# Layer 0 of a two-layer network on Trainium2: all columns of the transform matrices in x's first two steps

## The chip, the cores and the metric

The kernel runs on one core of a Trainium2 chip. The metric is the device time of one execution in microseconds (us), the median of a few runs. A profile of one further execution gives the start and end of every instruction on the engines: TensorE (PE matmuls, PEld weight loads), VectorE (DVE), ScalarE (ACT), GpSimd (POOL) and SyncE (SP, which issues most transfers), and the clock that was granted to TensorE.

## The reference

The input x is 4 batches of 32 images (times) of 128 x 128, in float32. Layer 0 is a convolution in Fourier space with an attention over the 32 times of a batch, two more spectral layers and several normalizations; layer 1 is an attention over 1024 tokens of 128 channels and a mixture of experts. Only the start of layer 0 bears on this case: x is normalized by groups of channels (`_gn`) and by image (`_inorm`), and the low modes of its two-dimensional Fourier transform are taken:

```
xn = _inorm(xa, norm1_w, norm1_b)
X = jnp.fft.rfft2(x, norm='forward')
Xk = jnp.concatenate([X[:, :, :mh, :mw], X[:, :, -mh:, :mw]], axis=2)
Yk = jnp.einsum('bixy,ioxy->boxy', Xk, w)
...
scores = jnp.einsum('bntk,bnsk->bnts', qf, kf) / (np.float32(np.sqrt(Hs * Ws)) * temperature)
p_attn = jax.nn.softmax(scores, axis=-1)
```

The keys, queries and values of the attention are spectral convolutions of the same image, so that their scores can be formed from the modes of x.

## The kernel before

**Transforms as matmuls.** A transform of an image is two matmuls with constant matrices. In the first step (`half_rows`, L285) the image is the stationary operand, 128 x 128, and the moving operand is `rows`, a matrix of 128 columns: 64 cosines and 64 sines of the frequencies 0 to 31 and -32 to -1. As the input is real, frequencies 0 to 32 are enough, and the step takes the first 33 columns of each half, 66 in all (L293). Four images go into one PSUM tile `pz`; ScalarE copies 32 columns of each half to `z` (L297) and the 33rd to `z32` (L298), and after two such tiles adds a constant to one column (L589). In the second step (`columns_of`, L495) two images' parts of `z` are the stationary operand, 128 x 128, and the moving operand is `colg`, cosines and sines of 33 frequencies along the other axis, times the group scale: 101 columns, of which the step takes the first 68 (L502). Four such matmuls fill the PSUM tile `it`, which ScalarE copies to `fold` (L507). `edge_row` (L562) takes other columns of `colg` for `z32`. All operands are float32.

**The stages of `spectra_of_images` (L481).** The 32 images of a batch are four groups of eight. For each group come two `pz` tiles, their copies, and then the second step of the group before. After the second step of two groups `unfold` (L509) makes the modes of 16 images: matmuls `em` (L521) and `std` (L532, L535), from which VectorE writes `xe`, `xm` (L537), two rows of biases (L544, L545) and `xx` (L548). `image_weights` (L465) makes the scale of each image: the sum `my` on TensorE, then a root (the helper `inv_std`, ScalarE at L248 and L251, VectorE at L247 and L252 to L255). After it comes `attention_weights` (L645): ScalarE copies `xe` to PSUM as `xp` (L655), VectorE and GpSimd form products `pa` and `pb` (L685, L687), and TensorE sums them (`so` L669, `sp` L700).

**What stands beside it.** For batch 0 these stages run alone at the start of the kernel, behind the loads of x and the group sums (`rows8`, L398; `bg`, L380), with the preparation of weights on VectorE: `value_weights` (L605 to L619) and the weights of keys and queries, `w_re` and `w_im` (L819 to L834). ScalarE also makes a selection matrix, `picked` (L628). For batches 1 to 3 they run at the end of the batch before, behind the second mode multiplication of its spectral layers (`spectra`, L1084: first step `pz` L305, second step `px` L1106, the multiplication on VectorE at L1117 and L1120 and its sum on GpSimd at L1123; ScalarE negates a part of it at L1068). Between them stand the coefficients of that batch's last normalization (`coefficients`, L1257): energies on VectorE (L1074, L1082), two sums `ms` on TensorE (L380), and two roots, r1 and rm, on ScalarE and VectorE, with short VectorE operations from L1266 to L1284.

**Order.** Layer 1 has a schedule written by hand (L1842). Layer 0 hasn't: a scheduler gives the instructions of each engine their order from its own estimates of their times, from the order of the program, and from the dependences that `behind` adds by hand. An engine then takes its instructions in that order. `pz` and the sums `my` share two PSUM buffers (tag "a"), `it` and others two (tag "b"), `em` and `std` two of double size (tag "wide").

Of the kernel before, what the change touches and what calls it, by code (L numbers as in the profile page):

```python
# [7 lines left out]
F32 = mybir.dt.float32  # L8
# [5 lines left out]
P = 128  # L14
B, T, H, C = 4, 32, 128, 128
NH = 32
KX, KY = 64, 33
KA = 17
KP = 9
GI = 8  # L20
# [76 lines left out]
NX = 2 + 3 * KY  # L97
# [33 lines left out]
def layer0(  # L131
    tc, x, kq_modes, kq_mirror, v_modes, v_mirror, pcw, mcols, mrows, heads, heads_by_row, heads_row, small_row, by_p, inv_cols, dram, x1, first
):
    nc = tc.nc
# [7 lines left out]
    const, ps, images, values, modes = (p.__enter__() for p in pools + right)  # L142

    def behind(later, earlier):

        tc.add_manual_dep(
            later.ins,
            earlier.ins.name,
            mybir.DependencyInfo(mybir.DependencyClass.NoSync, mybir.DependencyReason.DATA),
            reason="order",  # L150
        )
# [25 lines left out]
    def columns(n):  # L177
        at[0] += n
        return cst[:, at[0] - n : at[0]]

    rows = columns(128)
# [103 lines left out]
    def half_rows(images, z, last):  # L285

        for k in range(0, GI, 4):
            pz = ps.tile([P, 4, 2, KY], F32, name="pz", tag="a")
            for j in range(4):
                mm = nc.tensor.matmul(  # L290
                    pz[:, j],
                    images[k + j],
                    rows.rearrange("p (r x) -> p r x", r=2)[:, :, :KY],  # L293
                    start=True,
                    stop=True,
                )
            nc.scalar.copy(z[:, k : k + 4], pz[:, :, :, :32])  # L297
            nc.scalar.copy(last[:, :, k : k + 4], pz[:, :, :, 32].rearrange("p t r -> p r t"))  # L298
        return mm
# [181 lines left out]
    def spectra_of_images(b, xt, normed, then=None):  # L481


        _, colg, shift, sv, _ = normed
        n = 1 + KY
# [5 lines left out]
        half = T // 2  # L491
        pairs = half // 2
        folded = {}

        def columns_of(g, z):  # L495

            if g % half == 0:
                folded[g // half] = grp.tile([P, pairs, 2 * n], F32, name="fold", tag="fold")
            it = ps.tile([P, GI // 2, 2 * n], F32, name="it", tag="b")
            for j in range(GI // 2):  # L500
                mm = nc.tensor.matmul(
                    it[:, j], z[:, 2 * j : 2 * j + 2].rearrange("p t r x -> p (t r x)"), colg[:, : 2 * n], start=True, stop=True  # L502
                )
                if g == GI and then is not None:
                    behind(mm, summing["ms"])
            k = g % half // 2
            nc.scalar.copy(folded[g // half][:, k : k + GI // 2], it)  # L507

        def unfold(a):  # L509

# [71 lines left out]
        for g in GROUPS:  # L582
            z = grp.tile([P, GI, 2, 32], F32, name="z", tag="z")
            made = half_rows([xt[:, g + t] for t in range(GI)], z, z32[:, :, g : g + GI])
            if g == 0:
                ysc, scaled = image_weights(sv, made)
            if g == GI and then is not None:
                then(made)
            nc.scalar.activation(z[:, :, 0, 0], z[:, :, 0, 0], AF.Identity, bias=shift)  # L589
            if waiting:  # L590
                columns_of(*waiting.pop())
            if g == 3 * GI:
                unfold(0)
            waiting.append((g, z))
        columns_of(*waiting.pop())
        edges = edge_row()
        unfold(1)
# [228 lines left out]
    for dst, a, c, op in (  # L826
# [3 lines left out]
        t = prep.tile(shape, F32, name="wt", tag="wt")  # L830
# [64 lines left out]
    for b in range(B):  # L895
# [49 lines left out]
        for x0 in range(0, KX, NK):  # L945
# [3 lines left out]
            for i in range(4):  # L949
# [16 lines left out]
                for k in range(2):  # L966
# [11 lines left out]
                    for j in range(4):  # L978
# [4 lines left out]
                            start=i == 0 and k == 0,  # L983
                            stop=i == 3 and k == 1,
# [20 lines left out]
        for y0 in range(0, KY, 8):  # L1005
            n = min(8, KY - y0)
            py = ps.tile([P, 8, 2, T], F32, name="py", tag="b")
            for k in range(n):
                for part in range(2):
# [4 lines left out]
                        start=True,  # L1014
                        stop=True,
# [209 lines left out]
        for g in range(1, 4):  # L1225
            gelu(1, g)
            h, k = divmod(4 * g - 4, GI)
# [781 lines left out]
```

## Time and profile before

| | us |
|---|---|
| runs (3) | 2968.66, 2972.97, 2974.31; median 2972.97 |
| the profiled execution's own time | 2970.21 |
| its span, first to last instruction | 2968.5 |
| layer 0, to the first work of layer 1 on its path | about 850 |
| mean granted clock of TensorE | 0.979 |

The page shows TensorE busy for 2754.0 us (93% of the span), ScalarE for 2323.7, VectorE for 2187.5 and GpSimd for 2028.2. Most of it is layer 1, which starts near 830 us and which the change does not touch. So the busy shares of the whole say little here; what counts is which engine each stage of layer 0 waits for. In the list of groups each line has source line, engine, operation, output and inputs with their shapes, the count, busy time and mean of one in ns, and then the idle time ahead of them with what ended it. A float32 matmul stands there as two records. The chain of waits gives start, length and name of each piece of the path that ended last.

### The profile page before, as it was taken

The page shows a single profiled execution, that of the slowest core. Times are in us where ns is not written, and L with a number is a line of the kernel's source. Part 1 is how long each engine was busy: PE and PEld are TensorE (multiplying, and loading weights), DVE is VectorE, ACT ScalarE, POOL GpSimd, SP SyncE. Part 2 cuts the span into 40 slices and gives each one's busy share as a digit, 9 for nine tenths or more (in the row PEclk, how much of TensorE's full clock was granted, in tenths as well). Part 3 has the DMA queues.
Part 4 walks back from the last instruction along what each step waited for, and adds up shares of the span by engine and source line. Part 5 has one row for each costly group of instructions (what it writes and reads, how often), then busy time and mean ns, then how long its engine had stood idle before and what let it go on. Part 6 is the DMA issues. An engine that isn't in the chain of part 4 may idle for free.

```text
span 2968.5 us, 52711 instructions
## 1 busy us (share of the span) xinstructions
PE 2754.0 (93%) x19506; PEld 1364.1 (46%) x19506; DVE 2187.5 (74%) x4934; ACT 2323.7 (78%) x3235; POOL 2028.2 (68%) x1801
## 2 busy tenths in 40 slices
PE   8888988988878999999899999989999999999997
PEld 5465564664644443344444343444444343444443
DVE  4876787778866677775678688667778766878877
ACT  3554555456359999899899999989999998999991
POOL 1703605417208987878987878898787889798773
PEclk8998999999989999999999999999999999999998
DMA  3403304205021101002010100111010020000000
GB/s 93 126 1 70 117 1 106 81 9 152 14 61 33 33 1 40 8 16 57 1 26 15 26 15 8 42 25 31 15 26 15 10 56 15 26 13 21 15 15 14
DMA packets 151154, 107.72 MB, mean 36 GB/s; under 512 B 36303, under 2 KB 140018, under 8 KB 150898
## 3 DMA queue, kind: packets, MB, share of 16 engines
q1 hardware_dynamic: 147633, 102.26, 13.3%
q8 instruction: 154, 2.52, 0.4%
q10 hardware_dynamic: 3264, 2.10, 0.3%
q14 instruction: 103, 0.84, 0.1%
HBM read 63.86 MB, written 19.50 MB: 28 GB/s over the span
## 4 chain that ended last, share of the span: by engine, by line
PE 60%; POOL 12%; ACT 11%; DVE 10%; issue 6%; DMA 0%; POOLq 0%; DVEq 0%; ACTq 0%
PE d L1799 20%; PE po L1818 11%; PE px L1705 6%; ACT r L1849 5%; PE n L1799 4%; POOL e L1858 3%; PE po L909 3%; POOL e L1857 3%; POOL u L972 2%; ACT e L1865 2%; DVE r L1854 2%; POOL kx L1464 2%; PE pz L305 2%; DVE xc L1709 1%; PE px L1106 1%
## 5 line engine op out<-in xcount | busy, mean ns | idle before, releaser
L1854 DVE TENSOR_TENSOR r<-n,r 128x1024 f32<-128x1024 f32 (+1 forms) x1056 | 961.5, 952 | 478.6 <-PE n L1799 391.1
L1857 POOL TENSOR_TENSOR e<-r 128x512 f32<-128x512 f32 x528 | 674.0, 1277 | 270.2 <-DVE r L1854 269.6
L1849 ACT ACTIVATE r<-d 128x1024 f32<-128x1024 f32 (+1 forms) x1056 | 793.4, 803 | 64.7 <-PE n L1799 56.8
L1861 ACT ACTIVATE r<-r 128x1536 f32<-128x1536 f32 x528 | 783.6, 1484 | 16.7
L1858 POOL TENSOR_TENSOR e<-e,r 128x512 f32<-128x512 f32 x528 | 671.6, 1272 | 41.4
L1799 PE MATMUL d<-qe,ke 32*128 32x512 f32 (+3 forms) x2304 | 606.4, 602 | 39.4 <-ACT r L1849 35.0
L1818 PE MATMUL po<-e,kx 128*128 128x512 f32 (+3 forms) x1152 | 594.8, 605 | 17.4 <-POOL e L1870 17.4
L1799 PE MATMUL n<-qe,ke 32*128 32x512 f32 (+3 forms) x2304 | 606.3, 602 | 0.0
L1799 PE MATMUL n<-qf,kf 32*128 32x512 f32 (+3 forms) x2304 | 553.1, 555 | 0.0
L1799 PE MATMUL d<-qf,kf 32*128 32x512 f32 (+3 forms) x2304 | 551.8, 555 | 0.0
L1709 DVE SCALAR_TENSOR_TENSOR xc<-px,wgt,xc 128x128 f32<-128x128 f32 x1024 | 358.0, 350 | 42.1 <-PE px L1705 10.6
L1865 ACT ACTIVATE e<-e 128x512 f32<-128x512 f32 x528 | 325.8, 617 | 66.6 <-POOL e L1858 65.7
L1818 PEld LDWEIGHTS po<-e,kx 128*128 128x128 f32 x1152 | 175.8, 188 | 395.2 <-issue 309.7
L1799 PEld LDWEIGHTS d<-qe,ke 32*128 32x128 f32 x2304 | 176.6, 183 | 358.8 <-ACT r L1849 339.1
L1799 PEld LDWEIGHTS d<-qf,kf 32*128 32x128 f32 x2304 | 220.5, 186 | 175.7 <-issue 163.4
L1705 PE MATMUL px<-we,x2t 128*128 128x512 f32 x512 | 265.7, 605 | 6.7 <-DVE xc L1709 5.5
L972 POOL TENSOR_TENSOR u<-xb,gb 128x858 f32<-128x858 f32 (+1 forms) x112 | 219.7, 1994 | 56.9 <-PE po L909 53.3
L1799 PEld LDWEIGHTS n<-qf,kf 32*128 32x128 f32 x2304 | 228.3, 185 | 19.5 <-issue 11.7
L1123 POOL TENSOR_TENSOR spec<-part,part 128x512 f32<-128x512 f32 x16 | 25.3, 1578 | 304.0 <-DVE part L1120 110.8
L976 DVE TENSOR_TENSOR u<-xw,gb 128x858 f32<-128x858 f32 (+1 forms) x208 | 214.8, 1101 | 5.1 <-PE po L909 2.9
L1799 PEld LDWEIGHTS n<-qe,ke 32*128 32x128 f32 x2304 | 177.6, 183 | 9.4 <-DVE r L1854 0.9
L909 PE MATMUL po<-u,pr 128*32 128x429 f32 (+1 forms) x1280 | 150.4, 525 | 27.3 <-POOL u L972 17.7
(421 smaller groups left out, 3398.5 us busy)
## 6 DMA issues: line engine op xcount, KB each, us to landing
xb<-xd SPq DMA_DIRECT2D x128, 214.5 KB
xc<-x SPq DMA_DIRECT2D x29, 512.0 KB
x<-x SPq DMA_DIRECT2D x16, 512.0 KB
qf<-qe SPq DMA_DIRECT2D x64, 128.0 KB
out<-xc SPq DMA_DIRECT2D x15, 512.0 KB
x<-in_x SPq DMA_DIRECT2D x14, 512.0 KB
xb<-xd SPq DMA_DIRECT2D x32, 198.0 KB
kf<-ke SPq DMA_DIRECT2D x32, 128.0 KB
```

The source lines that it names most:

```text
L909: mm = nc.tensor.matmul(*args, **kw)
L972: weighed = nc.gpsimd.tensor_tensor(u, xb, gk, ALU.mult)
L1705: nc.tensor.matmul(px, x2t[:, k * P : (k + 1) * P], we[:, e0 : e0 + 4], start=True, stop=True)
L1709: nc.vector.scalar_tensor_tensor(xc[:, k], px[:, e], wgt[:, k, e0 + e : e0 + e + 1], xc[:, k], ALU.mult, ALU.add)
L1799: nc.tensor.matmul(o, k, q, start=turn == 0 or g > 0, stop=turn == 1 or g > 0)
L1818: nc.tensor.matmul(sums[c, h][:, q0 : q0 + c1 - c0], kx[:, jb], e[:, c0:c1], start=jb == 0, stop=is_last and q0 > 2 * P, skip_group_check= ...
L1849: nc.scalar.activation(r[:, g], d, AF.Ln, scale=1.0 / DSCALE)
L1854: nc.vector.tensor_tensor(r[:, g], part, r[:, g], ALU.mult)
L1857: nc.gpsimd.tensor_tensor(e, r[:, 1], r[:, 2], ALU.add)
L1858: nc.gpsimd.tensor_tensor(e, e, r[:, 0], ALU.add)
L1861: nc.scalar.activation(r, r, AF.Exp, scale=-1.0)
L1865: nc.scalar.activation(e, e, AF.Exp)
```

## The change

The first step takes all 128 columns of `rows`, and the second all 101 columns of `colg`. The tiles `pz` and `it` grow to hold them. The copies take the same elements as before: from `pz` the columns 0 to 31 and 32 of each half, from `it` the first 68 of 101 columns.

```diff
     def half_rows(images, z, last):
 
         for k in range(0, GI, 4):
-            pz = ps.tile([P, 4, 2, KY], F32, name="pz", tag="a")
+            pz = ps.tile([P, 4, 2, KX], F32, name="pz", tag="a")
             for j in range(4):
                 mm = nc.tensor.matmul(
                     pz[:, j],
                     images[k + j],
-                    rows.rearrange("p (r x) -> p r x", r=2)[:, :, :KY],
+                    rows.rearrange("p (r x) -> p r x", r=2),
                     start=True,
                     stop=True,
                 )
...
-            it = ps.tile([P, GI // 2, 2 * n], F32, name="it", tag="b")
+            it = ps.tile([P, GI // 2, NX], F32, name="it", tag="b")
             for j in range(GI // 2):
                 mm = nc.tensor.matmul(
-                    it[:, j], z[:, 2 * j : 2 * j + 2].rearrange("p t r x -> p (t r x)"), colg[:, : 2 * n], start=True, stop=True
+                    it[:, j], z[:, 2 * j : 2 * j + 2].rearrange("p t r x -> p (t r x)"), colg, start=True, stop=True
                 )
...
-            nc.scalar.copy(folded[g // half][:, k : k + GI // 2], it)
+            nc.scalar.copy(folded[g // half][:, k : k + GI // 2], it[:, :, : 2 * n])
```

As the scheduler's estimates depend on sizes, the order of instructions changes too, on TensorE, VectorE and ScalarE, in the stages named above and nowhere else; GpSimd's and SyncE's stay. In batch 0 VectorE's work for `w_re` and `w_im` (L820 to L834) comes ahead of the first `xe` (L537) instead of between its rows, and ScalarE's root of the image scale ahead of the second copy of group 1. In batches 1 to 3 ScalarE's part stands so (batch 2, from the two programs' lists; g0 to g3 are the groups of images, a and b their two tiles):

```
before: copies g0a g0b | copy g1a | fold g0 | negation L1068 | copy g1b | copy g2a | root n1 | copy g2b | root r1 | fold g1 | copies g3a g3b | fold g2 | xe L547 | root rm | fold g3
after:  copies g0a g0b | negation L1068 | copy g1a | fold g0 | root n1 | copy g1b | copy g2a | root r1 | copy g2b | fold g1 | copy g3a | root rm | copy g3b | fold g2 | xe L547 | fold g3
```

On TensorE the two sums `ms` stand after the first tile of group 2 instead of inside the last tile of group 3, and on VectorE most of the coefficients ahead of the first `xe` of the batch instead of between its rows.

## The prediction

> **What bounds the kernel now.** I read the page first, then the list of groups with shapes kept apart, then the chain of waits over layer 0 (the first 860 us of 2968.5), and last the busy time of each engine in stretches of 3.41 us, because the granted clock of TensorE moves in that step.
>
> The changed instructions are small. In the group list they stand beside a neighbour of the same weights with 128 columns:
>
> ```profile
> L305 PE MATMUL pz<-cst,q 128*128 128x128 f32 x256 | 36.5, 285 | 1.4 <-ACT z L225 1.4
> L290 PE MATMUL pz<-cst,x 128*128 128x66 f32 x256 | 39.1, 312 | 2.1 <-ACT z L298 2.0
> L290 PEld LDWEIGHTS pz<-cst,x 128*128 128x128 f32 x256 | 36.8, 227 | 4.4 <-ACT z L298 3.0 <-issue 1.4
> L501 PE MATMUL it<-colg,z 128*128 128x68 f32 x128 | 19.6, 306 | 0.0
> ```
>
> 128 images give 256 records at L290 and 64 pairs give 128 at L501: each f32 matmul is two passes. 66 columns cost no less than 128 (312 against 285 ns of one). The chain of waits says where they are on the path; nearly all of it is in batch 0:
>
> ```profile
> 22.45 3.43 PE pz L290 x16
> 26.40 1.97 PE pz L290 x8
> 28.37 1.71 PE it L501 x8
> 30.08 5.12 PE pz L290 x24
> 35.20 1.71 PE it L501 x8
> 36.91 3.41 PE pz L290 x16
> 40.32 1.71 PE it L501 x8
> 42.03 1.17 PE em L521 x32
> ```
>
> 24 passes in 5.12 us are 213 ns each; in batch 3 the weight loads of 32 passes start at 647.84 and the next matmul's at 651.41, 112 ns each. The factor is the clock. Columns of the next view: length of the stretch, then busy us and instructions of PE, PEld, DVE, ACT, POOL, then PEclk.
>
> ```profile
> 21.66:25.07 3.41, 3.28 (x16) 3.31 (x16) 2.20 (x13) 0.44 (x2) 0.00 (x0) 0.50 0.00 0
> 25.07:28.48 3.41, 3.30 (x16) 3.11 (x15) 2.15 (x11) 0.79 (x4) 0.00 (x0) 0.50 0.00 0
> 38.72:42.14 3.42, 3.42 (x21) 3.29 (x23) 0.00 (x0) 1.16 (x6) 0.00 (x0) 0.50 0.00 0
> 42.14:45.55 3.41, 3.41 (x42) 2.36 (x40) 2.24 (x9) 2.54 (x4) 0.00 (x0) 0.50 0.00 0
> 45.55:48.96 3.41, 3.15 (x52) 2.67 (x53) 2.74 (x12) 0.59 (x2) 0.00 (x0) 1.00 0.39 60
> 632.64:636.06 3.42, 3.41 (x16) 3.41 (x17) 2.10 (x10) 0.00 (x0) 0.00 (x0) 0.50 0.01 2
> 636.06:639.47 3.41, 3.41 (x39) 2.48 (x39) 2.88 (x6) 0.66 (x2) 0.00 (x0) 1.00 0.02 5
> ```
>
> From 21.66 to 45.55 us, seven stretches, TensorE runs at half clock although it is busy throughout. In batch 3 one such stretch is enough. The two are alike but for one thing: 21.66:25.07 holds 2 passes of bg (L380) and 14 of L290 with 66 columns; 632.64:636.06 holds 2 passes of bg and 14 of L305 with 128 columns. After the second the clock is full; after the first it stays at half.
>
> [...] half-clock stretches are 1, 2, 3, 4 or 7 times 3.41 us. [...] The trace has 112 ns a pass at full clock, 213 at half: [...]
>
> **The change, part by part.**
>
> Matmul time: 128 matmuls at L290 and 64 at L501, each two passes. New pass 112 ns at full clock and 213 at half, as L305 has with 128 columns; 101 lies between. Cost 0. [...]
>
> Copies at L297, L298, L507: same elements, other strides in PSUM (33 to 64, 68 to 101). L297, which already reads with strides, takes 375 ns for 256 elements a partition, L507, contiguous today, 390 for 272. I take 0; at 30 ns for each of 80 copies it would be 2.4 us, mostly beside TensorE. [...]
>
> The clock in batch 0, the main term. With 128 columns 21.66:25.07 becomes the twin of 632.64:636.06: [...] So the clock is full from 25.07. Until then 13.2 of L290's 64 passes are done. Before em (L521) follow 50.8 of L290, 24 of L501 and 2 of my: 76.8 x 0.112 = 8.6 us, plus 0.5 us where group 1 waits for the copies of group 0 (0.45 in batch 1). em starts at 34.2, not 41.96. Behind it I laid the new order end to end with the old durations. VectorE's order in the changed program has the w_re/w_im work (L820 to L834, about 3.5 us), which today stands between the xe rows, ahead of xe: its earlier work ends near 32.0 (today's 3.5 us from 32.73, brought forward because ACT's new order does n_r behind the first copy of group 1), so xe follows at 35.5, today 43.26. ACT copies picked (L628, 2.13 us) from 34.8 to 36.9, then xe's tail, then the last fold by 37.6; em of the second half ends near 38.6, xe at 38.7, xm and the bias rows to 39.3, xp on ACT to 39.9, the first pa (L685) at 39.95. Today it starts at 49.71: 9.8 us gained, and the chain from there to 82 us is TensorE back to back, so it moves along. No transfer holds it: DMA is at 0.00 to 0.02 from 21.66 to 45.55.
> Another execution has another phase. The rise falls between 24.8 and 28.2; at 28.5 I get 8.4, at 31.9, [...] 6.7. I take 9.0.
>
> The order of batches 1 to 3, which the instruction lists of both programs show to move; POOL and SP keep theirs. On ACT the negation L1068, which waits for POOL's spec (L1123), now stands ahead of group 1's first copy instead of behind a later one; on TensorE the two sums ms stand after 9 to 12 fewer matmuls; on VectorE nearly all of the coefficients (L1266 to L1281) come ahead of the first xe. The first costs: POOL ends at 238.08, 443.54, 646.63, the copy could start at 238.37, 442.91, 645.56, so with 0.6 us of L1068 TensorE stalls about 0.4, 1.0 and 1.5 us. Against it, today's own stall before group 2 (0.67 us in batches 2 and 3) goes, and the sums come 1 to 2 us earlier, with them the root r and rm, on whose ACT round trip VectorE waits 1.1 + 0.6 us in batch 2. Laid end to end, the last xe comes at 251.6, 456.3, 659.6 for 251.26, 456.96, 659.61, and the bias rows after it are no longer mixed with cq: pa moves by -0.1, -0.8, -0.2. I take -1.1, between -3 and +4 (stalls kept, gains lost).
>
> Sum: 2970.2 (the profiled execution's own time; span 2968.5) - 9.0 - 1.1 = 2960.1. The median of the runs, 2972.97, is 2.8 above that execution; with it 2963.
>
> **Rivals.** What this measurement can tell from no change is 0.2%, 5.9 us.
> (A) The clock rises one or two windows into batch 0: 2963. For: the twin windows. [...]
> (B) [...] the clock stays at half: only the order is left, 2972. [...] Against: L305 alone raised it in batch 3.
> (C) Slower: ACT's negation. If the stall ahead of group 1's copy (0.4 to 1.5 us) isn't absorbed by the earlier sums, and the roots r and rm, now ahead of the last copies of groups 2 and 3, hold TensorE too, each of three batches loses 2 to 3 us; with a clock as in B that is 2980. It decides from 2.0 us a batch. For: these waits are new. Against: the sums are the later end in batches 2 and 3 today.
> (D) The clock rises, but VectorE, with 3.5 us of w_re ahead of xe, or ACT's picked is slower than laid out, and half of the gain is lost: 2968.
>
> **How the numbers follow.** A 0.70, B 0.15, C 0.09, D 0.06. Predicted 2963. The range takes A with its phases (gain 12 [...] to 6.7), D and the nearer half of B: 2956 to 2972. Faster by over 0.2% is A: 0.70; within: B and D, 0.21; slower: C, 0.09.
>
> **What would show it.** PEclk 1.00 in most of 26 to 42 us; L290 passes of 112 ns from group 1 on; the first pa in batch 0 near 40 us; L290 and L501 with the old mean at equal clock. Wrong if the clock stays at 0.50 to 40 us, if a pass takes more than 112 ns at full clock, or if the first pa of batches 1 to 3 comes over 1.5 us later within its batch.

## The result, and the profile after

The changed kernel takes 2957.74 us (median of 6 runs, 2956.24 to 2960.34); the kernel before took 2973.64 us beside it (2968.66 to 2978.81). The ratio is 0.995, with a 95% interval of 0.9937 to 0.9963: 11 to 19 us faster. The two profiled executions, 2957.97 and 2970.21 us, are 12.2 us apart.

The chain of waits of the changed kernel in batch 0 follows (start us, us, what; "..." marks pieces left out). From the first L290, at 21.75 us, to em it needs 12.7 us; the kernel before needed 19.7.

```profile
21.96 3.53 PE pz L290 x16
...
25.52 0.37 ACT z L297
...
26.01 1.34 PE pz L290 x8
...
29.11 1.81 PE pz L290 x16
30.92 0.87 PE it L501 x8
31.80 1.81 PE pz L290 x16
33.60 0.87 PE it L501 x8
34.48 0.75 PE em L521 x29
```

16 passes of L290 take 1.81 us here and took 3.41; em starts at 34.4 us and started at 41.96. The next view is the busy time by stretches of 3.41 us, called windows from here on. Its columns are those of the prediction: length, then busy us and instructions of PE, PEld, DVE, ACT and POOL, then PEclk.

```profile
19.59:23.00 3.41, 1.70 (x8) 1.73 (x9) 2.41 (x16) 0.27 (x2) 0.00 (x0) 0.50 0.00 0
23.00:26.42 3.42, 3.21 (x16) 3.02 (x16) 1.64 (x10) 1.16 (x5) 0.00 (x0) 0.50 0.00 0
26.42:29.83 3.41, 3.41 (x32) 3.41 (x32) 3.33 (x17) 1.83 (x8) 0.00 (x0) 1.00 0.02 5
29.83:33.24 3.41, 3.41 (x33) 3.41 (x33) 3.41 (x17) 1.99 (x8) 0.00 (x0) 1.00 0.01 2
```

After the first window that is filled with 128-column passes, 23.00 to 26.42 us, the clock is full, and a window holds 32 passes instead of 16. Before, seven windows in a row stayed at half clock, TensorE busy for 3.28 to 3.42 us of each. The groups of the changed instructions:

```profile
L290 PE MATMUL pz<-cst,x 128*128 128x128 f32 x256 | 36.4, 292 | 2.5 <-ACT z L298 2.4
...
L501 PE MATMUL it<-colg,z 128*128 128x101 f32 x128 | 17.2, 275 | 0.0
```

One of them is not dearer with more columns, but cheaper: 292 ns for 312 at L290 and 275 for 306 at L501. More of them run at full clock.

The two profiled executions can be divided at the first L305 of a batch, to see where the time went: up to that of batch 0 it took 169.38 us and takes 160.08 (-9.3); from there to that of batch 3, which holds the changed steps of batches 1 to 3, 612.57 and 609.82 (-2.75); the rest, nearly all of it layer 1, 2186.55 and 2186.33 (-0.2). So three quarters of the 12.2 us between the profiles is batch 0. The medians are 15.9 us apart; what the later batches gain, and why, is asked further below.

### The profile page after: what moved, and what is told of

Its sections match the earlier page's. It is cut to its first block, busy times and chain, and to the rows that moved or that the text cites. A ratio compares the mean times of both kernels' runs of the same rounds, so it can differ in the third digit from the quotient of the medians.

```text
span 2956.2 us, 52712 instructions
## 1 busy us (share of the span) xinstructions
PE 2744.5 (93%) x19506; PEld 1355.2 (46%) x19506; DVE 2190.2 (74%) x4934; ACT 2324.2 (79%) x3235; POOL 2026.8 (69%) x1801
## 3 DMA queue, kind: packets, MB, share of 16 engines
q8 instruction: 154, 2.52, 0.4%
## 4 chain that ended last, share of the span: by engine, by line
PE 61%; POOL 14%; ACT 11%; DVE 9%; issue 6%; DMA 0%; POOLq 0%; DVEq 0%; ACTq 0%
PE d L1799 20%; PE po L1818 11%; PE px L1705 6%; ACT r L1849 5%; PE n L1799 4%; POOL e L1857 3%; POOL e L1858 3%; PE po L909 3%; POOL u L972 2%; ACT e L1865 2%; POOL kx L1464 2%; PE pz L305 2%; DVE r L1854 1%; PE px L1106 1%; DVE xc L1709 1%
## 5 line engine op out<-in xcount | busy, mean ns | idle before, releaser
L1799 PE MATMUL d<-qe,ke 32*128 32x512 f32 (+3 forms) x2304 | 606.1, 602 | 39.8 <-ACT r L1849 35.5
L909 PE MATMUL po<-u,pr 128*32 128x429 f32 (+1 forms) x1280 | 150.2, 525 | 27.2 <-POOL u L972 17.7
```

The source lines that it names most:

```text
L909: mm = nc.tensor.matmul(*args, **kw)
L1799: nc.tensor.matmul(o, k, q, start=turn == 0 or g > 0, stop=turn == 1 or g > 0)
```

## The experiments

Each run was timed beside the kernel before on the same chip, and ratios are to that. Four runs split the change.

**First step alone.** Only the two edits in `half_rows`; `columns_of` as before.

> Only the first step (L290) takes all 128 columns; the second (L501) keeps 68. Theory 1, the clock: [...] TensorE is at full clock from the second or third window of batch 0, the first pa starts at 40 to 42 us, and the time is that of the whole change: ratio to before 0.9935 to 0.9965. Theory 2, the reordering in batches 1 to 3 or the second step brings the gain: the first pa stays at 49 to 50 us and the ratio is 0.998 to 1.001.

Ratio 0.9955 (0.9942 to 0.9967), 2958.62 us. In the busy time by windows the clock rises after the second one in batch 0:

```profile
20.67:24.08 3.41, 2.12 (x10) 2.15 (x11) 2.71 (x18) 0.00 (x0) 0.00 (x0) 0.50 0.00 0
24.08:27.49 3.41, 3.20 (x16) 3.01 (x16) 1.67 (x11) 1.16 (x5) 0.00 (x0) 0.50 0.00 0
27.49:30.91 3.42, 3.42 (x32) 3.42 (x32) 3.16 (x16) 1.80 (x8) 0.00 (x0) 1.00 0.02 7
```

The first pa is at 41.41 us. As far as the intervals tell, the first step's columns bring the whole gain: the ratio of the whole change was 0.9937 to 0.9963.

**Second step alone.** Only the three edits in `columns_of`.

> Only the second step (L501) takes all 101 columns; the first (L290) keeps 66. Theory 1, the clock: [...] TensorE stays at half clock to about 42 us, first pa at 48 to 51 us, ratio 0.9985 to 1.0015. Theory 2, any more streaming at all (or the second step's order) brings it: pa at 40 to 45 us, ratio under 0.997.

Ratio 0.9994 (0.9986 to 1.0002), first pa at 49.53 us. Its windows in batch 0 stay at half clock, up to the one in which em runs (the last line here, with 42 matmul records); after that one the clock is full.

```profile
28.23:31.64 3.41, 3.41 (x17) 3.41 (x18) 0.45 (x2) 0.83 (x4) 0.00 (x0) 0.50 0.00 0
38.47:41.88 3.41, 3.41 (x19) 3.23 (x19) 0.00 (x0) 1.16 (x5) 0.00 (x0) 0.50 0.00 0
41.88:45.29 3.41, 3.41 (x42) 2.37 (x42) 2.07 (x8) 2.63 (x4) 0.00 (x0) 0.50 0.00 0
```

TensorE is busy for all 3.41 us of the first two, and the clock stays at 0.50 all the same. Being busy was not enough here; what was missing are the first step's columns.

**Batch 0 alone, and batches 1 to 3 alone.** The number of columns depends on the batch:

```
+        full = b == 0          # the other run: b > 0
+        nx = NX if full else 2 * n
-            pz = ps.tile([P, 4, 2, KY], ...
+            pz = ps.tile([P, 4, 2, kx], ...     # kx: KX if full else KY
```

The first has the changed kernel's order of VectorE's and ScalarE's instructions in batch 0 and that of before in the other batches; the second has the reverse.

> All columns in batch 0 alone; batches 1 to 3 have the columns and the order of before. Theory 1, the clock of batch 0 is the gain: first pa at 40 to 42 us, batches 1 to 3 at the lengths of before, ratio 0.9945 to 0.997 (9 us by the trace, more if the median of before has a worse phase than its profile). Theory 2, the order of batches 1 to 3 brings at least half: ratio 0.998 to 1.000.

> Batch 0 as before; all columns, and the new order, in batches 1 to 3. Theory 1: TensorE at half clock to about 42 us in batch 0, first pa at 48 to 51 us; in batches 1 to 3 the new order costs 0 to 1 us ahead of each pa, and what the changed kernel's profile shows to be won behind it (2.0, 1.2 and 1.05 us) is fewer half-clock windows by their phase: ratio 0.9985 to 1.0010. Theory 2, the order brings at least half: ratio 0.9975 or less.

Batch 0 alone: 0.9972 (0.9962 to 0.9983), first pa at 40.88 us, the first L305 at 160.44 us: the 9 us of the trace, the ratio a shade above the range given. Batches 1 to 3 alone: 0.998 (0.9974 to 0.9987), first pa at 50.76 us; TensorE stays at half clock in batch 0 for 34.1 us. Neither theory's range holds this ratio: it is more than the nothing of the first and less than the half of the second, and its interval touches both. By medians the two gains are 8.9 and 4.9 us, together 13.8. The whole change, timed apart from these two, gained 15.9 us, between 11 and 19 by its interval, so the two parts account for it within the noise.

**Is it the clock?** This run is the kernel before, with its 66 and 68 columns, and seven matmuls more whose result nobody reads. They stand where TensorE waits for bg's operand:

```
+    warm = ps.tile([P, 512], F32, name="warm", tag="b")
+    def keep_warm(earlier, tiles):
+        for k in tiles:
+            mm = nc.tensor.matmul(warm, rows, loaded[:, 4 * k : 4 * k + 4], start=True, stop=True)
+            behind(mm, earlier)
+    keep_warm(ahead[-1], range(1))
...
+    keep_warm(summing["mg"], range(1, 7))
```

> The kernel before, with its 66 and 68 columns, and seven f32 matmuls of 512 columns more in batch 0 whose result nobody reads: one behind the row sums, six behind the group sum mg, in the stretch in which TensorE waits for bg's operand (19.2 to 21.8 us). Theory 1, the clock: it no longer falls ahead of L290, and [...] it stays full; a pass takes 112 ns with 66 columns too, em starts at 32 to 34 us, the first pa at 38.5 to 41.5 us, batches 1 to 3 as before: ratio 0.9955 to 0.9978. Theory 2, the gain is in the wide columns or in the order of the later batches: pa at 48 us or later, ratio 0.999 to 1.001.

13 runs fell into two groups, 6 of 2959.76 to 2964.67 and 7 of 2969.16 to 2974.02 us; the ratio of all is 0.9987 (0.9978 to 0.9996), slower than the range given. The profiled execution, 2962.03 us, is of the first group. The first view has its windows. The second, from the timeline of TensorE (start us, us, engine, line, op, operands, count), has the six added matmuls (12 records) and the first records of L290:

```profile
20.82:24.23 3.41, 3.41 (x10) 1.50 (x9) 3.13 (x22) 0.00 (x0) 0.00 (x0) 1.00 0.00 0
24.23:27.64 3.41, 2.93 (x22) 2.41 (x20) 2.89 (x13) 0.92 (x5) 0.00 (x0) 1.00 0.00 0
27.64:31.06 3.42, 3.41 (x31) 3.41 (x31) 2.18 (x10) 1.67 (x9) 0.00 (x0) 1.00 0.03 7
```

```profile
19.37 5.40 PE L813 MATMUL warm<-x,cst 128*128 128x512 f32 x12
...
24.77 0.50 PE L290 MATMUL pz<-cst,x 128*128 128x66 f32 x3
```

The clock is full throughout with 66 columns, a window holds 31 passes, and the first pa comes at 42.03 us although the six matmuls held L290 back to 24.77 us: 7.7 us won with the columns of before. The scheduler also moved some of VectorE's and ScalarE's work in batch 0 of this run. But from the first L290 to em, a stretch that follows TensorE's pace, it took 11.1 us instead of 19.7. That makes the clock the cause of what batch 0 gains. A pass of 512 columns takes 5.40/12 = 0.45 us, and the six end at 24.77 us, 3 us behind the wait in which they were to fit (19.2 to 21.8).

A further execution of the same kernel, traced in case it falls into the other group:

> A second look at the kernel before with seven warming matmuls, whose times fell into two groups. Theory 1: if this time is 2969 us or more, the trace has TensorE at half clock in a part of batch 0 between 24 and 42 us[...]; if it is under 2966 us, at full clock all through[...]. Rival: a time of 2969 us or more with the full clock in batch 0.

2962.04 us, full clock in all of batch 0: the first group again. So no trace shows the second group. The granted clock over a whole run points the way expected of it: 0.980 to 0.983 in the first group, 0.977 to 0.980 in the second, but it doesn't say where the clock was lost. The supposed cause was that with 66 columns the full clock falls in some executions and then stays at half, and that with 80 it doesn't fall. It was tested with 80 columns in batch 0's first step and the same seven matmuls:

> The kernel before with the seven warming matmuls, and 80 columns (2x40) for 66 in the first step of batch 0. The run with 66 columns and these matmuls fell into two groups of times (2959.8 to 2964.7 and 2969.2 to 2974.0 us). Theory 1: [...] one group, 2959 to 2966 us, ratio 0.9955 to 0.9980. Rival: the two groups come from something else in the run (the row sums, the later batches): two groups again, ratio 0.998 to 1.000.

0.9972 (0.9962 to 0.9982), 9 runs from 2961.81 to 2966.71 us, none near the second group. This fits the supposed cause; no trace shows it, and at how many columns a full clock would fall was not measured.

**How many columns raise it?** These runs take 96 and 112 columns in the first step of batch 0; the second step stays at 68.

```
-            made = half_rows([...], z, z32[:, :, g : g + GI])
+            made = half_rows([...], z, z32[:, :, g : g + GI], KY if b else 48)   # 56 in the other
```

> In batch 0 alone the first step takes 96 columns (2x48) for 66; all else as before. [...] Theory 1 [...]: TensorE stays at half clock to about 42 us, first pa at 47 to 51 us, ratio 0.9985 to 1.0015. Rival, [...] rise in the second to fourth window, pa at 40 to 44 us, ratio 0.9955 to 0.998.

> In batch 0 alone the first step takes 112 columns (2x56); all else as before. [...] Theory 1: the clock rises after the first window that holds 15 or more passes of L290, first pa at 40 to 44 us, ratio 0.9955 to 0.9978. Rival as in the run with 96 columns (nothing turns between 96 and 112): both alike.

96 columns: ratio 1.0 (0.9991 to 1.0009), first pa at 49.28 us. 112 columns: 0.9979 (0.9972 to 0.9985), first pa at 44.81 us, both just outside the ranges given. Windows of the run with 96, then of the run with 112:

```profile
31.37:34.78 3.41, 3.41 (x17) 3.41 (x17) 3.19 (x15) 1.26 (x6) 0.00 (x0) 0.50 0.02 5
38.20:41.61 3.41, 3.41 (x18) 3.40 (x16) 0.00 (x0) 1.15 (x5) 0.00 (x0) 0.50 0.00 0
```

```profile
28.16:31.58 3.42, 3.42 (x19) 3.42 (x17) 2.48 (x12) 1.51 (x7) 0.00 (x0) 0.50 0.02 7
31.58:34.99 3.41, 3.41 (x17) 3.41 (x17) 3.41 (x16) 0.83 (x3) 0.00 (x0) 0.50 0.00 0
34.99:38.40 3.41, 3.41 (x33) 3.41 (x32) 0.39 (x2) 2.05 (x9) 0.00 (x0) 1.00 0.00 0
```

With 112 the clock rises to 1.00 after the window from 31.58, which holds 17 passes, almost all of L290; after the earlier ones, mixed with bg, waits or L501's 68 columns, it stayed at 0.50. With 96 it stays at 0.50 up to the end of em's window, at 45.02 us. The rise with 112 was expected a window sooner. Each of these is one traced execution: of the 13 runs with 96 columns two took 2959.46 and 2965.53 us, at a granted clock of 0.981 and 0.979 where the others have 0.975 to 0.978. In those the clock may have risen earlier; they are not traced.

**Where do 4.9 us in batches 1 to 3 come from?** Eleven of the 14 traces have these batches either as before (seven) or with all of the first step's columns (four). The table has means of the stretches, each summed over the three batches; a batch here runs from one batch's first L305 to the next one's. "Last sc" is the end of the last matmul of `sod` and `qk` into the scores `sc` (L715).

| stretch | as before, us | with the columns, us | difference |
|---|---|---|---|
| first L305 to first L290 | 192.73 | 193.39 | +0.66 |
| first L290 to first pa (the reordered one) | 59.07 | 57.60 | -1.47 |
| first pa to last sc | 31.23 | 30.02 | -1.21 |
| last sc to first L909 | 80.70 | 78.62 | -2.08 |
| first L909 to next L305 | 249.69 | 248.98 | -0.71 |

The seven are before, batch 0 alone, 96, 112, and the three traces with added matmuls and 66 or 80 columns; the four are changed, first step alone, batches 1 to 3 alone, and the changed kernel with added matmuls. The sums of the seven run from 612.0 to 616.3 us, those of the four from 606.1 to 609.9. Behind pa no instruction differs in kind. What differs is the clock: from the first pa to the last sc 4.4 us stand at half clock against 0, from there to L909 17.6 against 12.0. Windows of batch 1, before and then after:

```profile
250.35:253.76 3.41, 1.58 (x32) 1.00 (x22) 2.50 (x12) 0.52 (x1) 1.41 (x2) 1.00 0.60 84
253.76:257.18 3.42, 3.10 (x47) 1.93 (x50) 2.69 (x7) 2.84 (x7) 0.80 (x1) 0.50 0.48 66
270.83:274.24 3.41, 0.00 (x0) 0.00 (x0) 0.92 (x2) 3.41 (x9) 3.41 (x2) 1.00 0.08 30
274.24:277.66 3.42, 2.52 (x3) 1.17 (x4) 0.34 (x2) 2.22 (x5) 3.27 (x3) 0.50 0.26 24
277.66:281.07 3.41, 3.41 (x10) 1.01 (x8) 1.91 (x8) 0.18 (x1) 3.41 (x3) 0.50 0.41 53
```

```profile
241.46:244.87 3.41, 2.04 (x41) 1.36 (x40) 1.70 (x7) 0.73 (x2) 1.41 (x2) 1.00 0.57 86
244.87:248.28 3.41, 3.06 (x71) 2.51 (x75) 3.41 (x8) 2.80 (x7) 0.81 (x1) 1.00 0.54 57
261.94:265.35 3.41, 0.00 (x0) 0.00 (x0) 0.90 (x2) 3.41 (x10) 3.33 (x3) 1.00 0.12 45
265.35:268.76 3.41, 3.28 (x4) 1.17 (x4) 1.10 (x4) 1.62 (x4) 3.33 (x3) 0.50 0.40 36
268.76:272.18 3.42, 3.42 (x19) 1.42 (x22) 2.38 (x10) 0.00 (x0) 3.42 (x2) 1.00 0.27 40
```

Two things are to be seen. The window in which pa starts (252.95 and 244.09 us) holds 32 matmuls before and 41 after, and only after the first does the clock fall; whether the columns or the place of the window made that difference is not separated. And 7 us behind the last sc TensorE idles for 4.37 us in both kernels, more than a window long; in all 42 batches of the 14 traces the clock falls there. When the work resumes at the window's start (265.48 in 265.35:268.76), one window at half clock follows. When it resumes 0.9 us into it (275.14 in 274.24:277.66), TensorE is busy for 2.52 us of that window and a second follows. In these two traces the stretch from the last sc to L909 takes 26.03 to 26.07 us with one window at half clock (four batches) and 27.23 and 27.26 with two, 1.2 us more. Whether it was one or two went with the place at which the last sc ends in its window: over these 42 batches, an end at 1.83 to 2.78 us into the window gave one window in all 20 cases, every other place found (2.86 to 3.27 and 0.04 to 0.42) two in all 22. With the first step's columns 10 of 12 batches fall into the good places, as before 6 of 21.

To try this, the changed kernel with the first pa of batches 1 to 3 made twice:

```
+                if b and k == yy == 0:
+                    nc.vector.tensor_tensor(t, steps(row, [1, T], [1, nd]), other, ALU.mult)
```

> The changed kernel with the first pa product of batches 1 to 3 made twice: 0.7 us more on VectorE behind the reordered stretch. Theory 1, windows: in batches 1 to 3 the shorter stretch to pa puts what follows early enough in its window that only one half-clock window (3.4 us) falls into the stretch behind sc, [...]; 0.7 us later it is two (6.8 us) in most batches, so each batch loses 0.7 + 1.2 = 1.9 us where that happens: 2 to 6 us in all, ratio to before 0.9955 to 0.9975. Rival: the order alone makes the gain, each batch loses only its 0.7 us: ratio 0.9950 to 0.9960, one half-clock window behind sc in all three batches.

0.9969 (0.9956 to 0.9981), 2962.86 us. Between the last xe and the end of sc it costs only 0.33 us a batch. Behind sc the half clock lasts 6.8, 3.4 and 6.8 us instead of 3.4 three times, as the place of sc says (0.41, 2.53 and 2.91 us), which the rival had excluded. So here too the number of windows goes with the place; that the edit moved it there is not shown, since in batch 1 the place lies 1.4 us later than in the changed kernel and the edit makes 0.33 of them. The time itself decides nothing: in the profiled execution the first L305, ahead of every edited batch, comes 4.0 us later than in the changed kernel's, in part by half-clock windows at 82.9 and from 141.0 us that the changed kernel's trace doesn't have, and batches 1 to 3 are 1.1 us longer.

**Can it be made faster still?** One run is the changed kernel with the same seven matmuls. Another, whose edit stands here, has fewer of them in batch 0 and three ahead of bg in each later preparation:

```
+    keep_warm(ahead[-1], range(1))
+    sv = image_moments(ev)
+    keep_warm(summing["sb"], range(1, 2), 2)
+    moments = group_moments(sv)
+    keep_warm(summing["mg"], range(2, 5))
...
+            keep_warm(summing["d0"], range(3))
```

> The changed kernel with the same seven matmuls. Theory 1: the 6.8 us at half clock that the changed kernel still has in batch 0 go; L290 wins up to 3 us, of which the w_re work on VectorE and picked on ACT let 0.5 to 2 us through to the first pa (38.5 to 40.5 us); ratio to before 0.9930 to 0.9962. Rival: the extra matmuls delay bg or nothing reaches pa: 0.995 to 0.9975, pa at 40.6 us or later.

> The changed kernel, with matmuls whose result nobody reads in the idle stretches of TensorE: in batch 0 one of 512 columns behind the row sums, one of 256 behind sb and three of 512 behind mg; in each of the three next batches' preparations three of 512 behind d0, where TensorE waits 3.5 us for bg's operand. A 512-column f32 matmul takes 0.9 us (two records of 0.45, measured in the run with seven of them), so L290 of batch 0 starts at 21.7 to 22.2 us, not 24.2. Theory 1: no half clock in batch 0 and none of the 6.8 us ahead of each L290 in batches 1 to 3; first pa at 39.0 to 40.0 us (changed kernel: 40.6), 0.5 to 2 us less in each of the stretches from the first L305 to L290: ratio to before 0.9915 to 0.9950. Rival: in batches 1 to 3 these stretches hang on GpSimd and ACT, not on the matmuls' pace: 0.9945 to 0.9965.

0.9961 (0.9949 to 0.9974) with pa at 41.56 us, where the rival had it, and 0.9969 (0.9956 to 0.9981) with pa at 39.47, a ratio outside both ranges given. Neither is shown to be faster than the changed kernel. In the first the matmuls cost more ahead of L290 (24.22 for 21.75 us) than the clock brings behind it. The second brings pa 1.1 us forward, as expected, and yet the first L305 stays at 160.08 us. Its windows tell why:

```profile
76.79:80.20 3.41, 1.52 (x12) 0.16 (x8) 3.41 (x4) 1.04 (x2) 2.01 (x1) 1.00 0.41 134
80.20:83.62 3.42, 3.07 (x24) 1.32 (x28) 3.42 (x6) 1.08 (x2) 1.22 (x1) 0.50 0.40 128
```

The sparse start of the L909 stage (12 matmuls, 1.52 us) now fills one window, the clock falls, and L909 gives the 1.1 us back. In batches 1 to 3 the matmuls shift half-clock windows rather than remove them: between the first L305 and the first L290 the three batches have 27.3 us at half clock in both kernels, and they last 613.14 us for 609.82.

## Why the prediction was right

The forecast, rival A, held: 2963 us were forecast, 2957.74 measured, inside the range of 2956 to 2972 but near its lower end. The gain between medians was forecast at 10 us and measured at 15.9. B (only the order), C (slower) and D (half of the gain lost) are out.

- Matmul time, cost 0: right. From the timeline of weight loads, 16 L290 passes of the changed kernel start between 31.55 and the next matmul's 33.33 us, 111 ns each. In the run with the added matmuls a pass of 512 columns takes 0.45 us at full clock. By that rate 128 columns alone take 112 ns (an estimate, 0.45 us x 128 / 512), no more than the pass.
- Copies, 0: as taken. L297 takes 368 ns for 375, L298 170 for 173, L507 386 for 390.
- The clock in batch 0, 9.0 us: measured 9.3 in the profile, 8.9 by the medians of the run with batch 0 alone. The rise came at 26.42 us (24.8 to 28.2 forecast), em at 34.4 (34.2), xe at 35.30 (35.5), the first pa at 40.60 (39.95). The added matmuls ahead of the kernel before gave full clock and most of this gain without a column more, so that the cause holds and not the number alone.
- The order ahead of pa in batches 1 to 3, -0.1, -0.8, -0.2: the stretch from L290 to pa moved by +0.2, -0.9 and -0.8 in the profile, -1.5 in the means of several traces for -1.1 forecast.
- The term that was mis-sized is that of batches 1 to 3 as a whole: -1.1 was taken for everything, "pa moves by" so much and the rest moves along. It measured -2.75 in the profiled execution and -4.8 over the traces, as half-clock windows behind pa and behind sc went too (-1.2 and -2.1 us of it). Rival C's waits on ScalarE came to nothing that outweighs it.
- The step to the median, +2.8: mis-sized too. The changed kernel's median lies at its profiled time (2957.74 and 2957.97), so the gain between medians is larger than that between the profiles. Together: 0.3 us from batch 0, 1.7 from batches 1 to 3, 0.2 from the rest, 3.0 from this step make the 5.2 us missed.

Still open: what exactly raises the clock. In batch 0 it rose after a window with 16 matmul records and 128 columns in the first step (23.00:26.42 of the changed kernel) and after one with 17 records and 112 columns (31.58:34.99); it stayed at half after windows with 18 records, 16 of them L290, and 66 columns (31.90:35.31 of the kernel before) and with 17 records and 96 columns (31.37:34.78). So at like counts the columns went with the rise; a bound, and whether the columns alone decide, is not shown. Open too are the second group of times with 66 columns and the added matmuls, and whether the good places of sc come from the new order or are luck of this build: they are a matter of tenths of a microsecond.

## What to carry to other kernels

In this kernel a float32 pass of 128 columns took no longer than one of 66 (at half clock 213 ns each; at full clock 111 ns, and 110 ns with 66 by 31 records in 3.42 us), and in batch 0, where TensorE sat at half clock, the columns of the first step lifted it: look for stretches that are busy and at PEclk 0.50, and try there the columns that cost nothing. Price a saved microsecond only with the clock's windows behind it: here the place at which sc ended in its window went with one half-clock window more or less, 1.2 us, at the next idle stretch. A gain of a few microseconds in such a kernel should be read over several traces, not from one.

## What the runs showed of the hardware

TensorE busy for all of a window did not by itself raise its clock: in the traces with 66 or 96 columns a pass it stayed at 0.50 throughout those passes (23.9 us with 66 in the kernel before and with 96, 34.1 us in the run with batches 1 to 3 alone). With 112 it was at 1.00 after one window with 17 passes, almost all of L290 (34.99 us), with 128 after one with 16 (26.42 us in the changed kernel, 27.49 with the first step alone). With the seven matmuls ahead it stayed at 1.00 through the passes of 66 columns (24.23 to 34.47 us). An f32 matmul of 512 columns took 0.90 us at full clock, in two passes of 0.45. After the idle stretch of 4.37 us the clock was at 0.50 for one window when work resumed 0.13 us into a window (265.48 us in the changed kernel) and for two when it resumed 0.90 us into one (275.14 us before).
